# Slots taken behind the second sequence's last output product, constant rows made in the first stage, two expert loads inside the block stage

## The chip, the cores and the metric

The kernel runs on one core of one Trainium2 chip. The metric is device time in microseconds (us) of one execution. The kernel before has a median of 1152.28 us over three runs (1148.9, 1152.95, 1152.28). Engines are named as the profile names them: PE is TensorE (matrix products and transposes), PEld its weight loads, DVE is VectorE, ACT is ScalarE, POOL is GpSimd, SP is SyncE, which here only issues DMAs. A name such as "ACTq" is the same engine's queue of issued DMAs.

## The reference

The input x has shape (8, 512, 512): eight sequences of 512 tokens of width 512, all in float32. What is computed, cut to what matters:

```python
xn = layernorm(x)

# (a) lightning attention: 16 heads of 32, chunks of 128 tokens, a decay per head
q, k, v = rotary(silu(xn @ Wq)), rotary(silu(xn @ Wk)), xn @ Wv
per chunk:
    scores  = (q k^T) * D                      # D: decay inside the chunk, causal
    o       = scores v + (q * decay_q) S
    S       = lam_C * S + (k * decay_k)^T v    # state carried to the next chunk
gate = xn @ Wg1 @ Wg2
o    = o * sigmoid(gate)
o    = o * rsqrt(mean over each head of o^2 + eps) * norm_weight
s    = o @ Wo

# (b) mixture of experts over all 4096 tokens, 16 experts, top 4, hidden width 128
p     = softmax(xn @ gate_w.T);  keep the 4 largest, scaled to a sum of 1
mixed = sum over the 4 experts e of  p_e * (silu(xn Wg_e) * (xn Wu_e)) Wd_e
share = sigmoid(xn @ shared_gate_w) * swiglu(xn; sWg, sWu, sWd)
g     = silu(mixed + share)

out = x + s * g
```

## The kernel before

**Stages.** All of x is first normalised, and written to DRAM by token (`xn_d`) and transposed (`xT_d`). Every token is routed to four experts; an expert computes only its own tokens, in blocks of 128 that may hold tokens of any sequence. The stages in order of time are:

1. *First stage* (0 to about 226 us): `first()` (L999) runs the norm, the transposes, the router and the shared expert for all eight sequences, a piece at a time between the products of sequence 0 of the attention. `sort()` (L375) counts, and gives each of the 4 x 4096 choices its position in the lists of experts. It leaves `posi` (stored to `at_d`) and `sp` (the position's upper and lower part in float16).
2. *Table* (226 to about 302 us): beside sequence 1 of the attention, `table(room)` (L483) turns positions around: which token stands at each place of each of the 143 blocks. For each group of 16 choices DVE makes two one-hot tables, `place` and `block` (`make`, L529, L532, L535), by comparing a row of counting numbers `count` with `sp`; ACT scales half of the rows by the token's number (`number`, L543), DVE scales the other half by `half_token`. PE multiplies the two tables into `pn` (L566), and DVE adds the eight `pn` into `acc` (L575). At the end PE folds `acc` with the matrix `fold` into `pslot` (L582), and DVE makes the integer `slot` of it (L586). This is the list that the gathers read.
3. *Blocks* (about 321 to 710 us): 56 pairs of blocks and then 24 single blocks, always done (136 in all, `SURE`); up to 7 more stand in an If (L1280) behind them. For each block POOL gathers its 128 token rows by `slot` (L1112), SP transposes half of each row by DMA (`turn_rows`, L1119), PE the other half (`transpose_x`), ACT copies both into `xts` (`join`, L1138 and L1142; those of pair 0 by DVE), DVE copies the expert's weights to `wst` and the tokens' router weights to `w` (`prepare`, L1161, L1163), PE computes gate and up (`gate_up`, L1180, tile `pgu`), ACT the silu (L1192), DVE the product with up (L1193), PE the down product (`down`, L1211, tile `py`), DVE scales it (L1215) and SP stores it to `y_d` (L1216).
4. *Late stage* (about 710 to 1153 us): the attention of sequences 2 to 7. For each tile the four expert rows of a token are gathered from `y_d`, added up and multiplied in.

**Experts' weights.** `wexp` holds 16 experts of 768 KB each in SBUF. SP loads experts 0 to 10 at the start of the table stage (L1063). The room of the last five (`LATE`) is where the table works: one pair of `place` and `block` (`homes[0]`) in the room of experts 11 and 12, with `count` behind it, which reaches a little into expert 13's; the other pair in that of experts 14 and 15, with `half_token`, `fold` and `acc` behind it. So experts 11 to 13 are issued on SP when the table's last group is made (L556), each as the rows in its room are done with, and experts 14 and 15 on ACT's queue when the table is finished (L1077). Which expert a block reads is known only at run time, by a register (`of_block`, read from `eoff`), so an instruction that reads `wexp` counts as a reader of any expert.

**The turn from sequence 1 to the blocks.** `sequence(1, ...)` takes one step of the table at each `between[0]()`, called behind every product matmul of `value` (L618) and `product` (L662). With n == FIRST (2) its tail is: `gate_1(2)` (L629, PE, tile `pg`), `squares(1)` (L781 ACT squares, L784 PE sums, tile `pr`, L788 ACT square root), `inverse` (L792, DVE, `rs`), `value(2, 3)` (L615, tile `pv`) and `normed(1)` (PE spreads `rs` as `pb`, L801, and DVE scales the attention's output `on`, L806). What the table still has to do comes behind that. Then come the gathers of the first three pairs, `experts_of_blocks` (L1256 to L1263, six DVE operations that make `eoff`, in the room of `xts`), the four projections of sequence 1 (`project`, L813, tile `pw`, four tiles of four matmuls, 32 rows in the records), their copies (`spill`, L996 ACT, L997 store), and `begin(0, ...)` (L1218), which also issues `gate_2(2)` (L645) ahead of the first pair.

**Order.** The instructions of an engine are put in order by a scheduler, except where the code pins them: `on_pe()` (L208) places a matmul behind the one traced before it, and `behind(engine)` (L216) places an instruction behind the last one traced on that engine. `gone` is the list of DVE instructions that `prepare` is pinned to. SBUF comes from pools; a tile that takes the room of an older one waits for that one's readers. The pool `att` holds the tag `tmp` in `TMP` = 4 turns (`y`, `so`, `g1`, `rs` and the silu parts of q and k), and `v`, `kT`, `qT`, `xT`, whose room the blocks use again as `more`, `pls`, `wst` and `xts`. `p1` holds the first stage's tiles and is given up for `wexp`; `const` lives to the end. The gathered rows have six homes in turn, three `xg` of a pool of the blocks' own and three slices of `more`.

```python
    for t in range(NC):
        spill(FIRST - 1, t, project(FIRST - 1, t))
    on_of.pop(FIRST - 1)
    begin(0, lambda: gate_2(FIRST, banks="aakd"))
    by_dve.clear()
    blocks(range(len(items) + 2), aside)
```

## Time and profile before

| what | value |
|---|---|
| runs | 1148.9, 1152.95, 1152.28 us; median 1152.28 |
| profiled execution | 1155.04 us; its span, first to last instruction, 1153.2 us |
| mean granted TensorE clock | 0.99 of full |
| PE busy | 1117.9 us, 97% of the span, 7670 matmuls |
| DVE, ACT, POOL busy | 736.7, 429.3, 446.8 us (64, 37, 39%) |
| DMA | 218.49 MB, mean 189 GB/s |

By stage, from the table of busy time in stretches (us; the clock is the share of full speed that PE was granted):

| stretch | length | PE | DVE | ACT | POOL | clock | DMA engines' share |
|---|---|---|---|---|---|---|---|
| 0 to 226, first stage | 226 | 213.85 | 135.64 | 77.31 | 42.63 | 1.00 | 0.54 |
| 226 to 320, table | 94 | 82.50 | 66.76 | 36.69 | 12.39 | 0.93 | 0.62 |
| 320 to 710, blocks | 390 | 389.70 | 186.51 | 151.75 | 120.86 | 1.00 | 0.94 |
| 710 to 1153, late stage | 443 | 431.85 | 347.77 | 163.55 | 270.90 | 0.99 | 0.47 |

How to read it: the span is the profiled execution from its first to its last instruction; the execution itself was 1.84 us longer. A row of the trace in order of time begins with the start and the duration in us, then the engine, the line of the kernel, the operation, the tile written and the tiles read, the shapes and the number of instructions that the row joins; a bracket at its end is the engine's idle time just before it and what ended that. DMA rows under an engine's queue ("SPq", "ACTq", "POOLq") are the moments at which the engine issues them.

### The profile page before, as it was taken

Reading aid. Unit: us, or ns where it says so; the run is one execution under the profiler, and the core shown is the slowest. Engines: PE = TensorE matmul, PEld = TensorE weight load, DVE = VectorE, ACT = ScalarE, POOL = GpSimd, SP = SyncE. Lnnn points to the kernel's source line nnn. Section 1 sums busy time; section 2 is a strip of 40 time slices with the busy share of each in tenths; the row PEclk is TensorE's granted clock in tenths of the full one; section 3 lists DMA queues with packets and bytes.
Section 4 is the critical chain, followed back from the end, with each engine's and each line's share of the span. In section 5 each row is a group of like instructions: output and inputs, shape, how many; then the busy total and the mean of one; then the engine's idle time right before and its main releaser. Section 6 shows DMA issues by size and latency. Waiting matters only on the chain. (4 is left out here: it accounts for less than half of the span.)

```text
span 1153.2 us, 21330 instructions
## 1 busy us (share of the span) xinstructions
PE 1117.9 (97%) x7670; PEld 679.7 (59%) x7670; DVE 736.7 (64%) x1580; ACT 429.3 (37%) x927; POOL 446.8 (39%) x427
## 2 busy tenths in 40 slices
PE   7999999989899999999999999999999999999998
PEld 4445554445477777777777775555645545545554
DVE  6358734899334444555444445968879597697784
ACT  3223424154253333333333342353351522522541
POOL 3213100300233333333333322764877857958211
PEclk9999999989999999999999999999999999999999
DMA  9975431191799999999999994833737637434012
GB/s 338 319 276 194 156 127 47 51 352 40 217 200 236 220 244 238 238 241 237 253 233 234 272 215 178 323 101 108 254 116 230 183 108 244 150 122 145 29 36 75
DMA packets 163931, 218.49 MB, mean 189 GB/s; under 512 B 89840, under 2 KB 99184, under 8 KB 161776
## 3 DMA queue, kind: packets, MB, share of 16 engines
q1 hardware_dynamic: 142416, 145.18, 40.5%
q0 software_dynamic: 21120, 70.34, 23.9%
q10 hardware_dynamic: 288, 1.57, 0.4%
q8 instruction: 63, 1.03, 0.4%
q14 instruction: 44, 0.36, 0.1%
HBM read 126.78 MB, written 72.43 MB: 173 GB/s over the span
## 5 line engine op out<-in xcount | busy, mean ns | idle before, releaser
L1180 PE MATMUL pgu<-xts,wst 128*128 128x256 f32 x896 | 204.3, 381 | 0.0
L1180 PEld LDWEIGHTS pgu<-xts,wst 128*128 128x128 f32 x896 | 171.3, 191 | 46.7 <-issue 13.4
L1112 POOL DMA_INDIRECT xg<-xn_d,slot x69 | 65.7, 953 | 229.4 <-DVE w L1163 118.4
L1313 POOL DMA_INDIRECT yg<-y_d,place x128 | 142.5, 1113 | 31.1 <-issue 18.5
L1215 DVE TENSOR_SCALAR y<-py,w 128x512 f32<-128x512 f32 x136 | 101.6, 750 | 44.7 <-PE py L1211 31.0
L1211 PE MATMUL py<-wexp,slb 128*128 x272 | 129.9, 593 | 0.0
L615 PE MATMUL pv<-wv,xT 128*128 128x512 f32 x256 | 120.1, 610 | 3.1 <-DMA xT<-xT_d 2.0
L659 PE MATMUL pq<-xT,wq 128*128 128x512 f32 x256 | 118.2, 604 | 0.3 <-PEq L1278 0.3
L659 PE MATMUL pk<-xT,wk 128*128 128x512 f32 x256 | 118.2, 603 | 0.0
L1192 ACT ACTIVATE slb<-pgu 128x256 f32<-128x256 f32 (+1 forms) x80 | 28.1, 351 | 222.5 <-PE pgu L1180 184.1
L813 PE MATMUL pw<-wo,on 128*128 128x512 f32 x224 | 103.9, 612 | 5.8 <-DVE m L1351 5.8
L1193 DVE TENSOR_TENSOR slb<-slb,pgu 128x256 f32<-128x256 f32 (+1 forms) x80 | 30.5, 381 | 119.5 <-ACT slb L1192 118.1
L1112 POOL DMA_INDIRECT more<-xn_d,slot x67 | 63.5, 948 | 93.1 <-DVE w L1163 56.9
L1355 POOL TENSOR_TENSOR xo<-xo,m 128x512 f32<-128x512 f32 x31 | 45.3, 1460 | 131.2 <-DVE m L1351 123.3
L1142 ACT COPY xts<-pl 128x512 uint16<-128x512 uint16 x110 | 84.1, 767 | 9.0 <-DMA pl<-xg 9.0
L659 PEld LDWEIGHTS pq<-xT,wq 128*128 128x128 f32 x256 | 48.1, 193 | 55.3 <-issue 53.9
L748 DVE TENSOR_TENSOR sc<-ps,dmask 128x512 f32<-128x512 f32 x128 | 79.0, 676 | 0.9 <-PE ps L723 0.9
L615 PEld LDWEIGHTS pv<-wv,xT 128*128 128x128 f32 x256 | 46.3, 191 | 53.7 <-issue 47.1
L813 PEld LDWEIGHTS pw<-wo,on 128*128 128x128 f32 x224 | 42.5, 196 | 57.1 <-issue 47.7
L659 PEld LDWEIGHTS pk<-xT,wk 128*128 128x128 f32 x256 | 46.2, 189 | 50.7 <-issue 48.3
L1161 DVE COPY wst<-wexp 128x512 f32 x112 | 42.8, 424 | 39.8 <-DVE y L1215 18.7
L1211 PEld LDWEIGHTS py<-wexp,slb 128*128 128x128 f32 x272 | 45.5, 191 | 27.4 <-issue 26.8
(196 smaller groups left out, 1716.5 us busy)
## 6 DMA issues: line engine op xcount, KB each, us to landing
y_d<-y SPq DMA_DIRECT2D x136, 256.0 KB
wexp<-in_experts SPq DMA_DIRECT2D x14, 768.0 KB
sh_d<-sh SPq DMA_DIRECT2D x32, 256.0 KB
xT<-xT_d SPq DMA_DIRECT2D x8, 1024.0 KB
m<-sh_d SPq DMA_DIRECT2D x32, 256.0 KB
xo<-in_x SPq DMA_DIRECT2D x32, 256.0 KB
out<-xo SPq DMA_DIRECT2D x31, 256.0 KB
x<-in_x SPq DMA_DIRECT2D x7, 1024.0 KB
```

Of the source, the lines that this page charges most:

```text
L615: nc.tensor.matmul(pv, lhsT=xT_of[b][:, k, t * P : (t + 1) * P], rhs=wv[:, k, :], start=(k == 0), stop=(k == KC - 1))
L659: nc.tensor.matmul(ps, lhsT=w[:, k, g * P : (g + 1) * P], rhs=xT_of[b][:, k, :], start=(k == 0), stop=(k == KC - 1))
L748: nc.vector.tensor_tensor(s, pss[j].rearrange("p (c t) -> p c t", t=C), dmask[:, g * HG + j].unsqueeze(1).to_broadcast([P, NC, C]), ALU.mult)
L813: nc.tensor.matmul(pw, lhsT=on_of[b][:, g, t * P : (t + 1) * P], rhs=wo[:, g, :], start=(g == 0), stop=(g == G - 1))
L1112: nc.gpsimd.indirect_dma_start(out=row(i), out_offset=None, in_=xn_d, in_offset=bass.IndirectOffsetOnAxis(ap=slot[:, i : i + 1], axis=0))
L1142: (nc.vector.tensor_copy if j in by_dve else nc.scalar.copy)(xt[:, u, KP:, :].bitcast(U16).rearrange("p k (t h) -> p h k t", h=2), pls[j % ...
L1161: nc.vector.tensor_copy(to, wflat[:, bass.ds(off + u * KC * F, KC * F)])
L1180: nc.tensor.matmul(pg[:, o * 2 * P : (o + 1) * 2 * P], lhsT=wst[j % 2][k // KP][:, (k % KP * 2 + o) * F :][:, :F], rhs=xt[:, :, k, :], sta ...
L1211: nc.tensor.matmul(py, lhsT=hT[:, u * P : (u + 1) * P], rhs=wflat[:, bass.ds(off + KC * 2 * F, D)], start=True, stop=True)
L1215: gone.append(nc.vector.tensor_scalar(y, py, w[:, u : u + 1], None, ALU.mult).ins)
L1313: nc.gpsimd.indirect_dma_start(out=yg, out_offset=None, in_=y_d, in_offset=bass.IndirectOffsetOnAxis(ap=place[:, r, g : g + 1], axis=0))
L1355: nc.gpsimd.tensor_tensor(xo, xo, m, ALU.add)
```

## The change

- `TMP` goes from 4 to 5.
- `posi` moves from the first stage's pool to `const`. `count`, `half_token` and `fold` get tiles of their own in `const`, and are made on POOL in the first stage, behind `halves(0)`; the table no longer makes them (three ACT copies and the iota on POOL at its start) and no longer keeps them in `wexp`'s room.
- In the tail of sequence 1 four steps of the table are taken before `gate_1(2)`, and the next one behind it, so that the last `pn`, `pslot` and `slot` come behind the last output product; `slot` is pinned in DVE's order.
- `experts_of_blocks` moves ahead of `value(2, 3)` and `normed(1)`, works in the room of `wexp` from expert 14 on in place of `xts`, and is pinned in DVE's order. `prepare` is pinned behind the last scaling of `normed` (`scaled`).
- Experts 14 and 15 are no longer loaded on ACT's queue at the table's end; SP issues them inside the block stage, behind the gate and up of pairs 1 and 3 (`aside`).
- The homes of gathered rows swap halves, so that the first three are slices of `more`; the gathers are pinned on POOL, the DMA transposes chained in the order written, and the two copies of transposed halves in `join` pinned behind the copy before them.

```diff
--- before.py
+++ after.py
@@ -35,7 +35,7 @@
 
 NB = (B * N * TOPK + E * (P - 1)) // P
 WE = KC * 2 * F + D
-TMP = 4
+TMP = 5
 FIRST = 2
 NBQ = -(-NB // 4)
 
@@ -189,10 +189,13 @@
 
     wt = p1.tile([P, NT, E], F32, tag="wt", name="wt")
     sgs = p1.tile([P, NT], F32, tag="sgs", name="sgs")
-    posi = p1.tile([P, TOPK, NT], I32, tag="posi", name="posi")
+    posi = const.tile([P, TOPK, NT], I32, tag="posi", name="posi")
 
     sp = const.tile([P, 2, TOPK * NT], F16, tag="slot", name="sp")
 
+    count = const.tile([P, 2 * NB, QUAD], F16, tag="count", name="count")
+    half_token = const.tile([P, NT], F16, tag="half_token", name="half_token")
+    fold = const.tile([P, HALF], F16, tag="fold", name="fold")
     eoff = const.tile([P, 2, NBQ], I32, tag="eoff", name="eoff")
     end = const.tile([P, 2, E], F32, tag="end", name="end")
     filled = const.tile([P, 1], I32, tag="filled", name="filled")
@@ -497,7 +500,6 @@
                 flat.rearrange("p (u q j) -> p u q j", u=quads, j=QUAD))
 
         homes = [(part(quads, HALF, QUAD), part(quads, 2 * NB, QUAD))]
-        count = part(2 * NB, QUAD)
         free[0] = 2 * WE * (LATE - LATE // 2)
         homes.append((part(quads, HALF, QUAD), part(quads, 2 * NB, QUAD)))
 
@@ -505,13 +507,7 @@
             free[0] += n
             return half[:, free[0] - n : free[0]]
 
-        half_token, fold, acc = flat(NT), flat(HALF), flat(2 * NB)
-        nc.scalar.copy(half_token, token)
-        for h in range(0, P, HALF):
-            nc.scalar.copy(fold[h : h + HALF], ident[h : h + HALF, h : h + HALF])
-        nc.gpsimd.iota(
-            count, [[1, 2 * NB], [0, QUAD]], base=0, channel_multiplier=0,
-            allow_small_or_imprecise_dtypes=True)
+        acc = flat(2 * NB)
 
         def rows(of, n):
             return of.rearrange("p (u j) -> p u j", j=QUAD).unsqueeze(2).to_broadcast(
@@ -583,7 +579,8 @@
                     pt[h * HALF : (h + 1) * HALF, :NB], lhsT=fold,
                     rhs=acc.rearrange("p (b h) -> p b h", h=2)[:, :, h], start=True, stop=True)
         t = const.tile([P, NB], I32, tag="slot", name="slot")
-        nc.vector.tensor_scalar(t, pt[:, :NB], float(B * N // 2), None, ALU.add)
+        with behind(DVE):
+            nc.vector.tensor_scalar(t, pt[:, :NB], float(B * N // 2), None, ALU.add)
         slots.append(t)
 
 
@@ -791,6 +788,8 @@
     def inverse(b):
         nc.vector.reciprocal(rs_of[b], rs_of[b])
 
+    scaled = []
+
     def normed(b):
         pbs = [bank("a", f"pb_{b}_{c}") for c in range(NC)]
         rs = rs_of.pop(b)
@@ -803,8 +802,8 @@
                         rhs=rs[cq, :], start=True, stop=True)
         for c in range(NC):
             oc = on_of[b][:, :, c * C : (c + 1) * C]
-            nc.vector.tensor_tensor(
-                oc, oc, pbs[c].rearrange("p (g t) -> p g t", t=C), ALU.mult)
+            scaled[:] = [nc.vector.tensor_tensor(
+                oc, oc, pbs[c].rearrange("p (g t) -> p g t", t=C), ALU.mult).ins]
 
     def project(b, t):
         pw = bank("d", f"pw_{b}_{t}")
@@ -826,6 +825,27 @@
         by_token(b, 0)
         query(b, 1)
         step()
+
+    def experts_of_blocks():
+        half = NBQ * 2 * E
+        room = wflat[:, (E - LATE // 2) * WE :]
+        cm = room[:, :half].rearrange("p (b e) -> p b e", e=2 * E)
+        ef = room[:, half : half + NBQ]
+        ei = room[:, half + NBQ : half + 2 * NBQ].bitcast(I32)
+        with behind(DVE):
+            nc.vector.tensor_tensor(
+                cm, end.rearrange("p w e -> p (w e)").unsqueeze(1).to_broadcast([P, NBQ, 2 * E]),
+                iota_b.unsqueeze(2).to_broadcast([P, NBQ, 2 * E]), ALU.is_le)
+        with behind(DVE):
+            nc.vector.tensor_reduce(ef, cm, axis=AX.X, op=ALU.add)
+        with behind(DVE):
+            nc.vector.tensor_copy(ei, ef)
+        with behind(DVE):
+            nc.vector.tensor_scalar(ei, ei, E - 1, None, ALU.bitwise_and)
+        with behind(DVE):
+            nc.vector.tensor_scalar(eoff[:, 0], ei, float(WE), None, ALU.mult)
+        with behind(DVE):
+            nc.vector.tensor_scalar(eoff[:, 1], ei, float(D), None, ALU.add)
 
     def sequence(b, step, projected, before=None, defer=False, also=lambda: None):
 
@@ -867,9 +887,13 @@
             step()
         v_of.pop(b)
         if n == FIRST:
+            for _ in range(4):
+                next(filling)
             gate_1(n)
+            next(filling, None)
             squares(b)
             inverse(b)
+            experts_of_blocks()
             value(n, 3)
             normed(b)
             return
@@ -1026,6 +1050,15 @@
     turn(0)
     norm(1)
     halves(0)
+    with behind(POOL):
+        nc.gpsimd.tensor_copy(half_token, token)
+    for h in range(0, P, HALF):
+        with behind(POOL):
+            nc.gpsimd.tensor_copy(fold[h : h + HALF], ident[h : h + HALF, h : h + HALF])
+    with behind(POOL):
+        nc.gpsimd.iota(
+            count, [[1, 2 * NB], [0, QUAD]], base=0, channel_multiplier=0,
+            allow_small_or_imprecise_dtypes=True)
     xs_of.pop(0)
     load_x(3)
     pieces = first()
@@ -1069,12 +1102,8 @@
     next(filling)
     between[0] = lambda: next(filling, None)
     sequence(1, lambda: None, spill)
-    for _ in filling:
-        pass
     between[0] = lambda: None
     slot = slots[0]
-    for e in range(E - LATE // 2, E):
-        nc.scalar.dma_start(wexp[:, e, :], a["experts"][:, e, :])
     left.close()
 
 
@@ -1085,8 +1114,8 @@
     ROW = 2 * (D + E)
     HOMES = 6
     more = att.tile([P, 2 * NC * D], U16, tag="v", name="more", bufs=2)
-    homes = [blkp.tile([P, ROW], U16, tag=f"xg{j}", name=f"xg{j}") for j in range(HOMES // 2)]
-    homes += [more[:, j * ROW : (j + 1) * ROW] for j in range(HOMES // 2)]
+    homes = [more[:, j * ROW : (j + 1) * ROW] for j in range(HOMES // 2)]
+    homes += [blkp.tile([P, ROW], U16, tag=f"xg{j}", name=f"xg{j}") for j in range(HOMES // 2)]
     pls = [att.tile([P, 2, KC, P], U16, tag="kT", name=f"pl{j}", bufs=2) for j in range(2)]
     xts = att.tile([P, 2, 2, KC, P], F32, tag="xT", name="xts", bufs=1)
     wst = [
@@ -1099,6 +1128,7 @@
         {}, {}, {}, {}, {}, {}, [], [], [])
 
     by_dve = [0]
+    turned = []
 
     def inside(f):
         return lambda j: f(j, items[j]) if 0 <= j < len(items) else None
@@ -1109,14 +1139,17 @@
     @inside
     def gather(j, its):
         for i in its:
-            nc.gpsimd.indirect_dma_start(
-                out=row(i), out_offset=None, in_=xn_d,
-                in_offset=bass.IndirectOffsetOnAxis(ap=slot[:, i : i + 1], axis=0))
+            with behind(POOL):
+                nc.gpsimd.indirect_dma_start(
+                    out=row(i), out_offset=None, in_=xn_d,
+                    in_offset=bass.IndirectOffsetOnAxis(ap=slot[:, i : i + 1], axis=0))
 
     @inside
     def turn_rows(j, its):
         for u, i in enumerate(its):
-            nc.sync.dma_start_transpose(pls[j % 2][:, u], row(i)[:, D : 2 * D])
+            with tc.issue_after(turned[-1]) if turned else nullcontext():
+                turned.append(nc.sync.dma_start_transpose(
+                    pls[j % 2][:, u], row(i)[:, D : 2 * D]).ins)
 
     @inside
     def transpose_x(j, its):
@@ -1139,9 +1172,10 @@
             xt[:, :, :KP, :].rearrange("p u k t -> p u (k t)"),
             pt_of.pop(j)[:, : n * KP * P].rearrange("p (u kt) -> p u kt", u=n))
         for u in range(n):
-            (nc.vector.tensor_copy if j in by_dve else nc.scalar.copy)(
-                xt[:, u, KP:, :].bitcast(U16).rearrange("p k (t h) -> p h k t", h=2),
-                pls[j % 2][:, u].rearrange("p (h k) t -> p h k t", h=2))
+            with behind(DVE if j in by_dve else ACT):
+                (nc.vector.tensor_copy if j in by_dve else nc.scalar.copy)(
+                    xt[:, u, KP:, :].bitcast(U16).rearrange("p k (t h) -> p h k t", h=2),
+                    pls[j % 2][:, u].rearrange("p (h k) t -> p h k t", h=2))
         xt_of[j] = xt
 
     def on_dve(what, i, low, high):
@@ -1242,32 +1276,20 @@
                 down(j - 1)
 
     def aside(j):
+        if j in (1, 3):
+            e = E - LATE // 2 + j // 2
+            nc.sync.dma_start(wexp[:, e, :], a["experts"][:, e, :])
         if j == PAIRS:
             load_xT(FIRST)
 
     kept.clear()
 
-    def experts_of_blocks():
-        half = NBQ * 2 * E
-        room = xts.rearrange("p j u k t -> p (j u k t)")
-        cm = room[:, :half].rearrange("p (b e) -> p b e", e=2 * E)
-        ef = room[:, half : half + NBQ]
-        ei = room[:, half + NBQ : half + 2 * NBQ].bitcast(I32)
-        nc.vector.tensor_tensor(
-            cm, end.rearrange("p w e -> p (w e)").unsqueeze(1).to_broadcast([P, NBQ, 2 * E]),
-            iota_b.unsqueeze(2).to_broadcast([P, NBQ, 2 * E]), ALU.is_le)
-        nc.vector.tensor_reduce(ef, cm, axis=AX.X, op=ALU.add)
-        nc.vector.tensor_copy(ei, ef)
-        nc.vector.tensor_scalar(ei, ei, E - 1, None, ALU.bitwise_and)
-        nc.vector.tensor_scalar(eoff[:, 0], ei, float(WE), None, ALU.mult)
-        nc.vector.tensor_scalar(eoff[:, 1], ei, float(D), None, ALU.add)
-
     for j in range(3):
         gather(j)
-    experts_of_blocks()
     for t in range(NC):
         spill(FIRST - 1, t, project(FIRST - 1, t))
     on_of.pop(FIRST - 1)
+    gone += scaled
     begin(0, lambda: gate_2(FIRST, banks="aakd"))
     by_dve.clear()
     blocks(range(len(items) + 2), aside)
@@ -1279,6 +1301,7 @@
         items[:] = [(i,) for i in range(SURE, NB)]
         done.clear()
         gone.clear()
+        turned.clear()
         for j in range(3):
             gather(j)
         begin(0)
```

## The prediction on record

> **What bounds the kernel now.** The first part of the page has PE busy for 1117.9 of 1153.2 us (97%), and the chain that ended last runs mostly through PE. So I ask of each edit only where it moves a hole in PE's row, and what a hole costs behind it. I listed PE in order of time and looked for bracketed idle time, then read the engine named there, then the granted clock. These are PE's holes near the change (start, us, engine, line, tiles; the bracket is the idle time before and its releaser), with undisturbed rows of the same work for comparison:
>
> ```profile
> 237.35 0.90 PE L691 MATMUL pk<-ident,kT 128*128 128x128 f32 x3 [4.16 <-DVE state L738]
> 238.04 5.19 PE L659 MATMUL pq<-xT,wq 128*128 128x512 f32 x6
> ...
> 255.54 0.49 PE L691 MATMUL pk<-ident,kT 128*128 128x128 f32 x3
> 255.87 2.74 PE L659 MATMUL pq<-xT,wq 128*128 128x512 f32 x6
> ...
> 265.92 4.54 PE L615 MATMUL pv<-wv,xT 128*128 128x512 f32 x6 [2.02 <-DMA xT<-xT_d]
> ...
> 283.33 2.84 PE L615 MATMUL pv<-wv,xT 128*128 128x512 f32 x6
> ...
> 300.83 0.26 PE L582 MATMUL pslot<-wexp 128*64 128x143 f16 x2 [2.76 <-DVE on L806]
> 301.01 15.67 PE L813 MATMUL pw<-wo,on 128*128 128x512 f32 x32
> ...
> 319.88 1.15 PE L645 MATMUL p<-g,wg 32*128 32x128 f32 x26 [1.90 <-ACT so L996]
> 320.97 5.41 PE L1180 MATMUL pgu<-xts,wst 128*128 128x256 f32 x16
> ...
> 326.65 3.62 PE L1180 MATMUL pgu<-xts,wst 128*128 128x256 f32 x16
> ```
>
> Each of these four holes is paid twice: the same matmuls behind it take longer. In the table by stretches the granted clock reads 0.50 from 237 to 243 and from 267 to 270. Holes of 1.90 to 4.16 us cost 1.7 to 2.9 us behind them; one of 1.16 us at 868.87 cost nothing (its eight pw took the usual 3.70).
>
> The causes, on the other engines and queues:
>
> ```profile
> 226.21 3.24 POOL L512 IOTA wexp<- 128x572 f16 x1 [9.01 <-DMA at_d<-posi]
> ...
> 229.48 0.43 DVE L529 TENSOR_TENSOR wexp<-wexp,sp 128x512 f16<-128x512 f16 x1 [4.42 <-POOL wexp L512]
> ...
> 301.12 0.33 ACTq L1077 DMA_DIRECT2D wexp<-in_experts  x1
> 305.13 0.76 DVE L1161 COPY wst<-wexp 128x512 f32 x2 [2.17 <-DMA wexp<-in_experts]
> 318.01 1.38 ACT L1142 COPY xts<-pl 128x512 uint16<-128x512 uint16 x2 [7.53 <-DMA pl<-xg]
> ```
>
> The reader sees that the table's first DVE row waits for the iota, the iota for a store; and that the hole at 319 comes from ACT standing in a wait for a transpose with two evictions queued behind it. From 321 us on PE has no hole for 56 pairs of 5.61 us, with the DMA engines 0.93 busy (500 to 700 us): what the start of that stage gains or loses goes straight to the end.
>
> **1. Rows made early (gain 6.1).** DVE's last list cast ends at 225.06. The table then started at 229.48; without the iota, the three ACT casts and the store's release (posi now has a home of its own) it can start at 225.1, 4.4 earlier. Its ten operations take 7.1 us, so the state copies come at 232.2 instead of 236.5, ahead of PE, whose keys end at 233.18. The idle 4.16 goes, and with it 0.90-0.49 and 5.19-2.74, together 2.86 of slow clock: 7.0. What is late next: bank a for gate_2, freed by the eviction of the first pn, which on DVE stands behind kT and half of the next table rows. I get PE waiting until 240.2 for it, about 1.4 where it lost 0.6 before, so 0.9 back: 6.1 (bounds 5.0 and 7.0). The moved copies and the iota stand on POOL behind halves(0), some 4 to 5 us (3.24 for the iota); POOL is idle there for 5.83 us before 25.03, so they cost nothing; without that cover, at most the time by which the next rstd would be late, some 1 us.
>
> **2. A third expert ahead of xT (loss 2.8).** With count gone from the shared room, expert 13's load depends on no table row, and in the built program SP issues it ahead of sequence 2's xT. xT is wanted sooner too: PE's scores end at 257.8 (263.9 less 6.1). Expert 13 waits for expert 10's landing, which I put at 254.6 (257.2 less the 2.6 by which SP's fourth load comes forward). Both transfers, 1.84 MB, then go together: the three loads at 287.41 moved 2.36 MB in 7.1 us, which gives 5.8 for these, and about 1 us of older stores is in front, so xT lands near 262.1. The hole grows from 2.0 to 4.3; the slow clock behind it by 0.5, between the rows' 1.7 and 2.9. Bounds: 0 (xT lands 5.1 after its issue, as now) and 4.
>
> **3. Slots and norm behind the last po (gain 2.6).** Now, last po (289.13) to first pw (301.01) is 11.9 us. After: pn 1.15, pg 1.0, pslot 0.3, pr 1.0 on PE (3.4); ACT's table load and root end at 4.2; reciprocal 0.95; experts_of_blocks, now ordered ahead of the scaling, 1.36+1.35+4x0.18 = 3.4 (8.6); first scaled tile 0.6: pw starts at 9.3. PE's own work, pv 3.6 and pb 1.17, ends at 8.1, so a hole of 1.2 remains where 2.76 was. Expert 11 and 12's loads at table end come with the same shift.
>
> **4. The projections' clock (gain 1.9).** 15.67 for 32 pw against 32x0.43 = 13.74. The remaining hole of 1.2 is nearest to the row of 1.16, which kept its clock. Bounds 0 and 1.9.
>
> **5. No wait at gate_2 (gain 3.7).** slot is now ready about 2.8 us behind the last po instead of 13.6, so gathers and transposes have landed some 10 us before the projections end; ACT runs the four evictions first and DVE copies pair 0's transposes. The 1.90 goes and 5.41-3.62 = 1.8. If a transpose still were late here, the 3.7 would stay as it is.
>
> **6. Experts 14 and 15 inside the pairs (loss 7.2).** This is the new wait. The loads leave ACT's queue, where only DVE's 2.17 waited for them, and go to SP at blocks 1 and 3. The expert is chosen by register, so a reader of wexp behind such a load waits for it whole: in the built program the first py waits for 14's semaphore, and the third py, put in the middle of the fifth pair's pgu, for 15's. PE is in order, so all pgu behind wait too. From the first pgu: load 14 waits for pair 2's weight copies (3.45 for pgu 0, 0.6 for the copy) and is issued at 4.2. By the row at 301.12 such a load lands 3.6 us after its issue, at 7.9; py is due at 7.8. In front of it in SP's order are two transposes, beside it two pairs of gathers, so I add 1.7: a stall of 1.8, and 1.8 for the clock, as behind 1.90: 3.6. Bounds: 0.1, and 7.2 (landing 7.9 after the issue, as pair 0's transposes from 307.45 to 315.3, and 2.9 of clock). Load 15 waits for py of pair 1, then for y and pair 4's weight copies; two transposes and two stores of y precede it. It is issued about 10 us behind py 0, due 13 behind it: again 3.6, bounds 0.4 and 7.2. Behind SP's waiting load stand the transposes of pairs 4 and 7, due 10 us or more later. The rest (TMP of 5, order of the homes, transposes chained, ACT's copy order) lies beside PE: ACT waits 183.6 us for pgu in this stage, and PE's order is unchanged from pair 5 on. Bounds -2 and 1, at nothing: no PE row there names a tmp buffer.
>
> On the clock, the Trainium skill, "TensorE: Matmul & The Clock Gate", section "HAM oscillation — how this bites in real kernels", says that holes are dangerous above about 3.4 us. By that the stalls of 1.8 would keep their clock, but the slow rows behind 1.90 and 2.76 would not exist either; the trace shows them, and decides. By the page item 6 would be 3.6 and items 4 and 5 together 1.9, a sum of 4.2.
>
> **Sum.** 6.1-2.8+2.6+1.9+3.7-7.2 = 4.3 us earlier. The profiled execution took 1155.04 (span 1153.2 and 1.84 around it), so 1150.7 for it; the median shown is 2.76 lower, and I take the same off: 1152.28-4.3 = **1148.0**.
>
> **Rivals.** A, the loads land in time: item 6 is 0.5 instead of 7.2, gain 11.0, 1141.3. For it: 3.6 us at 301.12; against it: the DMA engines were free then and are 0.93 busy here. B, the gains are eaten: xT 4 late and both stalls near 3.2 with 2.4 of clock, gain 6.1-4+2.6+1.9+3.7-11.2 = -0.9, 1153. Also here: the table is DVE-bound (it has almost no idle time from 229 to 262), so item 1 comes out smaller. C, slower: the 1.57 MB, some 4 us of all DMA engines, don't fit into a stage with 0.4 us free per pair. Then transposes land late for six pairs or so, each a hole of 1.2 with up to 1.8 behind it: 4.3-18 = 13.7 later, 1166, down to 1158 if the clock holds. It decides once a transpose lands over 8 us after its issue (507.71, read from 515.7); now no pair waits for one.
>
> **Chances.** Forecast (1145 to 1150.5) 0.46, A (below 1145) 0.24, B 0.18, C 0.12. A change of 0.5%, 5.8 us, is about what a measurement of this kernel can tell from none: below 1146.5 lie A and 0.17 of the forecast: faster 0.41; slower, above 1158, C: 0.12; within 0.47. The ends: all best, 14.7 gained; items at their worst, 6 lost. The range 1140 to 1156 leaves out C and a third of A.
>
> **What would show it.** Item 1: no hole before L691 near 233, the iota before 25 us. 2: a hole of 4 us before pv near 262. 3: pslot about 2 us behind the last po, pw 9.3 behind. 4: 32 pw in 13.9. 5: the first pgu 2.6 behind the last pw and 3.6 long. 6: holes before the first and third py, released by wexp's loads, with slow rows behind. I am wrong if py waits for neither load, if xT lands by 260, or if holes come up in the steady pairs.

## The result, and the profile after

The changed kernel takes 1164.33 us (median of four runs, 1163.86 to 1168.53) against 1152.47 for the kernel before: ratio 1.0115, 95% interval 1.0088 to 1.0142. It is **slower by 12 us**, where 4.3 us less were forecast. Its profiled execution took 1164.48, with a span of 1162.7, so the two profiles to compare differ by 9.5 us.

PE's rows of the kernel after in order of time, those that answer to the ones shown of before (start, us, engine, line, tiles; in brackets the idle time before and its releaser; L812 is the L813 of before, L1214 the L1180, L1245 the L1211):

```profile
233.25 0.55 PE L688 MATMUL pk<-ident,kT 128*128 128x128 f32 x3 [0.24 <-DVE state L735]
...
264.86 5.49 PE L612 MATMUL pv<-wv,xT 128*128 128x512 f32 x6 [7.25 <-DMA xT<-xT_d]
...
288.08 1.08 PE L767 MATMUL po<-sc,v 128*32 128x128 f32 x32
...
291.26 0.26 PE L578 MATMUL pslot<-wexp,fold 128*64 128x143 f16 x2
...
298.61 14.00 PE L812 MATMUL pw<-wo,on 128*128 128x512 f32 x32 [1.34 <-DVE on L805]
...
314.72 3.69 PE L1214 MATMUL pgu<-xts,wst 128*128 128x256 f32 x16
...
327.48 3.75 PE L1245 MATMUL py<-wexp,slb 128*128 x4 [4.73 <-DMA wexp<-in_experts]
331.02 4.16 PE L1214 MATMUL pgu<-xts,wst 128*128 128x256 f32 x16
...
335.46 1.88 PE L1245 MATMUL py<-wexp,slb 128*128 x4
...
347.31 3.78 PE L1245 MATMUL py<-wexp,slb 128*128 x4 [4.35 <-DMA wexp<-in_experts]
...
654.37 2.07 PE L1220 MATMUL pgu<-wexp,xt 128*128 x4 [3.46 <-ACT xt L1176]
```

The reader sees: the hole ahead of the keys is gone; the one ahead of `pv` has grown from 2.02 to 7.25; `pslot` comes 2.1 us behind the last `po`, and the projections run at full clock; the pairs begin 6.25 us earlier than before (314.72 against 320.97). Then two `py` wait for `wexp`, and the matmuls behind them take twice their 1.88. A hole among the single blocks, at 654, is one nobody had reckoned with.

SP's queue tells when the loads were issued:

```profile
255.71 0.33 SPq L552 DMA_DIRECT2D wexp<-in_experts  x1
256.44 0.32 SPq L594 DMA_DIRECT2D xT<-xT_d  x1
...
316.75 3.49 SPq L1151 DMA_TRANSPOSE pl<-more  x2
320.34 0.53 SPq L1281 DMA_DIRECT2D wexp<-in_experts  x1
...
341.23 0.38 SPq L1281 DMA_DIRECT2D wexp<-in_experts  x1
```

Laid against each other, the two profiles give this account. "Pairs" runs from the first `pgu` to the first `pgu` of a single block, "singles" from there to the first `pq` of the late stage.

| step of the prediction | forecast | measured | from |
|---|---|---|---|
| 1, rows early | +6.1 | +6.3 | sequence 1's last scores end 257.61, before 263.90 |
| 2, expert 13 ahead of xT | -2.8 | -6.3 | the last `po` ends at 289.1 in both |
| 3, tail | +2.6 | +2.4 | first `pw` 298.61, before 301.01 |
| 4, clock of `pw` | +1.9 | +1.7 | 14.00, before 15.67 |
| 5, gate_2 | +3.7 | +3.9 | rest of the 6.25, and 3.69 for 5.41 |
| 6, two loads in the pairs | -7.2 | -14.5 | pairs 326.53, before 313.75 less that 1.72 |
| "the rest", at nothing | 0 | -6.5 | singles 81.61, before 75.14 |
| late stage, not in the sum | 0 | +3.5 | 439.84, before 443.34 |
| sum | +4.3 | -9.5 | |

The last row but one is no gain of the change: before's profiled execution had a hole of 2.61 us in the late stage with 5.34 for eight `pw` behind it, which is 1.15 and 3.70 after, and that execution was 2.8 us above its kernel's median. The fifth `tmp` buffer alone changes nothing (e10 below).

### The profile page after: what moved, and what is told of

Read it like the earlier page. It is cut to its first block, busy times and chain, and to the rows that moved or that the text cites. A ratio compares the mean times of both kernels' runs of the same rounds, so it can differ in the third digit from the quotient of the medians.

```text
span 1162.7 us, 21323 instructions
## 1 busy us (share of the span) xinstructions
PE 1117.9 (96%) x7670; PEld 679.6 (58%) x7670; DVE 738.6 (64%) x1580; ACT 437.0 (38%) x924; POOL 447.5 (38%) x430
## 5 line engine op out<-in xcount | busy, mean ns | idle before, releaser
L1214 PE MATMUL pgu<-xts,wst 128*128 128x256 f32 x896 | 204.2, 381 | 0.1
L1214 PEld LDWEIGHTS pgu<-xts,wst 128*128 128x128 f32 x896 | 171.3, 191 | 47.8 <-issue 27.0
L1143 POOL DMA_INDIRECT more<-xn_d,slot x69 | 66.0, 956 | 246.1 <-DVE w L1197 113.5
L1245 PE MATMUL py<-wexp,slb 128*128 x272 | 134.7, 611 | 9.1 <-DMA wexp<-in_experts 9.1
L656 PE MATMUL pq<-xT,wq 128*128 128x512 f32 x256 | 115.7, 593 | 0.3 <-PEq L1300 0.3
L812 PE MATMUL pw<-wo,on 128*128 128x512 f32 x224 | 100.6, 596 | 5.9 <-DVE m L1374 4.5
L1143 POOL DMA_INDIRECT xg<-xn_d,slot x67 | 63.3, 945 | 100.4 <-DVE w L1197 61.3
L1176 ACT COPY xts<-pl 128x512 uint16<-128x512 uint16 x110 | 76.7, 767 | 0.7 <-DMA pl<-more 0.7
L812 PEld LDWEIGHTS pw<-wo,on 128*128 128x128 f32 x224 | 41.2, 190 | 55.3 <-issue 45.2
L1245 PEld LDWEIGHTS py<-wexp,slb 128*128 128x128 f32 x272 | 46.7, 196 | 38.2 <-issue 33.3
```

Source lines behind the costliest of these rows:

```text
L656: nc.tensor.matmul(ps, lhsT=w[:, k, g * P : (g + 1) * P], rhs=xT_of[b][:, k, :], start=(k == 0), stop=(k == KC - 1))
L812: nc.tensor.matmul(pw, lhsT=on_of[b][:, g, t * P : (t + 1) * P], rhs=wo[:, g, :], start=(g == 0), stop=(g == G - 1))
L1143: nc.gpsimd.indirect_dma_start(out=row(i), out_offset=None, in_=xn_d, in_offset=bass.IndirectOffsetOnAxis(ap=slot[:, i : i + 1], axis=0))
L1176: (nc.vector.tensor_copy if j in by_dve else nc.scalar.copy)(xt[:, u, KP:, :].bitcast(U16).rearrange("p k (t h) -> p h k t", h=2), pls[j % ...
L1214: nc.tensor.matmul(pg[:, o * 2 * P : (o + 1) * 2 * P], lhsT=wst[j % 2][k // KP][:, (k % KP * 2 + o) * F :][:, :F], rhs=xt[:, :, k, :], sta ...
L1245: nc.tensor.matmul(py, lhsT=hT[:, u * P : (u + 1) * P], rhs=wflat[:, bass.ds(off + KC * 2 * F, D)], start=True, stop=True)
```

## The experiments

Theory S: the loss is made of waits, py's for the loads inside the pairs and pv's for xT. Rival T: the traffic of the loads costs, wherever it is put. Each group ran on one chip. On that of the first group the kernel before took 1152.5 us; on the four chips of the others 1163.4 to 1164.1, so there only ratios count. Most of that difference lies in the late stage, behind nearly all that is edited here: 439 to 444 us in the first group's profiles and in the two above, 451 to 458 in all others. A ratio is to the kernel before of the same group, with its 95% interval. From each profile, in us:

| kernel | ratio | first pgu at | pairs | singles |
|---|---|---|---|---|
| before | 1 | 320.97 | 313.75 | 75.14 |
| after | 1.0115 (1.0088 to 1.0142) | 314.72 | 326.53 | 81.61 |
| e1 loads on ACT | 0.9996 (0.9967 to 1.0025) | 318.95 | 312.03 | 75.22 |
| e2 xT first | 1.0091 (1.0065 to 1.0116) | 311.39 | 323.24 | 81.27 |
| e3 both | 0.9989 (0.9972 to 1.0006) | 317.90 | 312.03 | 76.08 |
| e4 traffic only | 1.0009 (0.9993 to 1.0024) | 319.21 | 312.03 | 77.11 |
| e5 xT first, loads on SP | 1.0004 (0.9985 to 1.0023) | 310.58 | 316.88 | 78.11 |
| e6 zeros behind xT | 0.9968 (0.9943 to 0.9994) | 310.63 | 318.19 | 79.92 |
| e7 tail alone | 0.9995 (0.9965 to 1.0025) | 317.73 | 313.69 | 75.28 |
| e8 loads at pair 20 | 1.0110 (1.0085 to 1.0135) | 315.28 | 327.65 | 77.92 |
| e9 loads on ACT, late | 1.0001 (0.9978 to 1.0025) | 312.63 | 315.43 | 79.70 |
| e10 before, TMP 5 | 0.9995 (0.9977 to 1.0012) | 319.33 | 314.40 | 75.14 |
| e11 orders undone | 1.0134 (1.0109 to 1.0158) | 325.18 | 323.72 | 75.14 |
| e12 after again | one run, 1183.77 us | 314.70 | 328.73 | 80.87 |
| e13 after, pin out | 1.0030 (1.0002 to 1.0057) | 312.84 | 326.27 | 76.29 |
| e14 before, pin in | 1.0038 (1.0004 to 1.0071) | 319.51 | 316.14 | 80.02 |
| e15 e9, pin out | 0.9897 (0.9842 to 0.9953) | 312.95 | 313.69 | 75.62 |
| e16 after, third profile | 1.0089 (1.0066 to 1.0112) | 313.85 | 323.16 | 82.28 |
| e17 before, other pin | 1.0043 (1.0013 to 1.0073) | 318.32 | 318.17 | 77.32 |
| e18 e15 again | 0.9929 (0.9905 to 0.9953) | 311.29 | 313.77 | 75.79 |

### Group 1: the stalls, xT and the traffic

e1: the two loads leave the pairs.

```diff
 def aside(j):
-    if j in (1, 3):
-        e = E - LATE // 2 + j // 2
-        nc.sync.dma_start(wexp[:, e, :], a["experts"][:, e, :])
...
 slot = slots[0]
+for e in range(E - LATE // 2, E):
+    nc.scalar.dma_start(wexp[:, e, :], a["experts"][:, e, :])
```

> Experts 14 and 15 go back to ACT's queue at the table's end; all else is the changed kernel. Theory S (stalls): the two waits of py for wexp (4.73 and 4.35 us) and the slow clock behind each are what the block stage lost; they go, 14.5 us less than the changed kernel's 1164.3, so 1150 (1147 to 1153). Theory T (traffic): the 1.57 MB cost their time wherever they are moved, by lateness of the transposes that follow; then holes appear at the first pairs instead and the time stays above 1157. The hole of 3.46 us among the single blocks: if it belongs to the change it is seen here too.

e2: expert 13 behind xT.

```diff
+with tc.issue_after(xT_load[FIRST]):
     nc.sync.dma_start(wexp[:, e, :], a["experts"][:, e, :])
```

> Expert 13's load is held behind the load of sequence 2's xT on SP; all else is the changed kernel. Theory S: xT lands some 5.1 us behind its issue as in the kernel before, the hole ahead of pv is near 4.4 instead of 7.25, and the slow clock behind it is shorter: 3 to 4.5 us less than the changed kernel, 1160.5. Rival: xT waits for the stores of zeros issued ahead of it, not for expert 13; then the hole stays above 6.5 and the time at 1164.

e3 is e1 and e2 together.

> Both edits together. Theory S: the gains add, 18 to 19 us below the changed kernel: 1146 (1143 to 1149), 6 us below the kernel before. Theory T: above 1155.

e4 is e1, and in `aside` at pairs 1 and 3 a load of the same bytes into DRAM, `nc.sync.dma_start(spare[j // 2], ...)`, pinned behind the last transpose.

> As the first of these, experts 14 and 15 on ACT's queue at the table's end, but two loads of the same size are issued by SP at the places where the changed kernel issues those of experts 14 and 15; they copy the same bytes to a room in DRAM that nobody reads, so no instruction waits for them (their result is not used). Theory S: no py hole; within 2 us of the first kernel, 1150 to 1152. Theory T: the traffic alone makes transposes late, 1157 or more.

Measured: e1 took 1151.53 (12.8 less than the changed kernel), e2 1161.16, e3 1149.91, e4 1153.98. In e1, e3 and e4 no py waits, and the pairs take 312.03 in all three, with the traffic and without: 326.53 - 312.03 = 14.5 is what the two waits cost. T falls: e4 is 0.0013 above e1, inside the intervals; its 1153.98 is 2 us over what S gave, and in its profile 1.9 of them stand among the single blocks, none in the pairs. e2 is 3.2 us under the changed kernel, as S gave; one of its py waits 3.69 for the load, at the other PE stands 3.89 where the profile names nothing that it waited for. e3 is above the 1143 to 1149 that S gave, since ACT's queue has a price of its own; ACT's rows of e1:

```profile
290.14 2.79 ACTq L1108 DMA_DIRECT2D wexp<-in_experts  x1
292.97 1.28 ACT L785 ACT_TABLE_LOAD   x1 [2.92 <-issue]
```

and PE's of the same:

```profile
263.73 5.12 PE L612 MATMUL pv<-wv,xT 128*128 128x512 f32 x6 [5.92 <-DMA xT<-xT_d]
...
295.76 1.17 PE L800 MATMUL pb<-rs,wge 16*128 16x128 f32 x32 [1.26 <-DVE rs L789]
299.85 16.98 PE L812 MATMUL pw<-wo,on 128*128 128x512 f32 x32 [2.92 <-DVE on L805]
```

The load's issue stood 2.8 us in front of the square root; the norm came late, and `pw` took 16.98 for 14.00. The hole ahead of pv is 4.88 in e2 and 5.50 in e3, 5.92 and 5.80 in e1 and e4: expert 13 explains only a part of the 7.25, 2.4 between the changed kernel and e2, 0.4 between e1 and e3.

### Group 2: where the rest of xT's wait comes from, and where a load may stand

e5 is e3 with `nc.sync` for `nc.scalar`. e6 is e5 with the stores of zeros behind xT:

```diff
-for i in range(SURE, NB):
-    nc.sync.dma_start(y_d[i * P : (i + 1) * P, :], none)
...
+for b in range(SURE, NB):
+    with tc.issue_after(xT_load[FIRST]):
+        nc.sync.dma_start(y_d[b * P : (b + 1) * P, :], zeros[0])
```

e7 is the kernel before with the tail's order and the two loads on SP at the table's end. e8 is the changed kernel with both loads in `aside` at `j == 20`.

> The changed kernel with expert 13 behind xT, and experts 14 and 15 issued by SP at the table's end instead of inside the pairs (before, with ACT's queue, the load stood ahead of ACT's square root and cost a hole of 1.3 ahead of pb, 1.6 more ahead of pw and 3.0 of slow clock). Theory: no hole ahead of pb, pw 14.0, no py hole; 5.9 us less than the same with ACT's queue (1149.9): 1144 (1141.5 to 1146.5). Rival: the two loads stand ahead of pair 0's transposes on SP and make pgu 0 late by some 4 us: 1148 or more.

> As e5, and the seven stores of zeros (1.84 MB) are issued behind xT too, from a tile of their own. Theory D: the DMA engines are full from 228 to 260 us, so xT can't land before what stands ahead of it has; without these stores it lands at 258 to 259.5 instead of 262.5, the hole ahead of pv is 1 to 2 us instead of 5, and the clock behind it is shorter: 4 us less than e5, 1140 (1137.5 to 1142). Rival: xT's landing is set by its own issue (it waits for PE's last reads of sequence 1's xT) and takes 5 us or more whatever is ahead: the hole stays above 4, the time within 1.5 us of e5.

> The kernel before with one part of the change alone: the order of the tail (last pn, pslot, slot directly behind the last output product, experts of blocks ahead of the norm), and experts 14 and 15 issued by SP at the table's end. The rows stay in the table. Theory: the tail's three terms, 2.4 + 1.7 + 3.9 = 8.0 measured between the two profiles, come without the early rows: 1152.5 - 8 = 1144.5 (1142 to 1147), and e5 is within 2 us of it, since the early rows alone only make PE wait longer for xT. Rival: the early rows are worth their 6 us, then this is 6 us above e5.

> The changed kernel with both loads issued one behind the other at pair 20 instead of pairs 1 and 3. Theory S: a py waits wherever the load is put; one hole near pair 21, as long as two loads take to land (8 to 10 us) less the some 3 us by which py is due later, so 5 to 7 and 2.5 of slow clock, and no py hole at the first pairs: 14.5 - 9 = 5.5 us less than the changed kernel, 1159 (1156 to 1161). Rival: the stalls belong to the crowded start of the stage; in its middle the loads land in time, no py hole, 1150.

PE and SP of e6, and then of e8 (two views each; the first row of each fence is PE's):

```profile
260.25 2.84 PE L617 MATMUL pv<-wv,xT 128*128 128x512 f32 x6 [2.88 <-DMA xT<-xT_d]
```

```profile
254.31 0.33 SPq L598 DMA_DIRECT2D xT<-xT_d  x1
254.69 4.72 SPq L553 DMA_DIRECT2D y_d<-none  x7
```

```profile
446.26 3.75 PE L1245 MATMUL py<-wexp,slb 128*128 x4 [7.52 <-DMA wexp<-in_experts]
```

```profile
436.38 1.16 SPq L1281 DMA_DIRECT2D wexp<-in_experts  x2
```

e6 has the hole at 2.88 without slow clock, where theory D gave 1 to 2 and its rival more than 4. Its ratio is 0.0036 under e5's (3.7 us by the medians), with intervals that overlap, and in the two profiles the first pgu comes at the same time, since PE stands 2.92 ahead of `pw` in e6 where the profile names nothing. So D has the direction, not the size: from issue to landing xT takes 5.94 us in e6 and 6.95 in e5. The stores ahead of xT were a part of its wait.

e8 shows py waiting 7.52 in the middle of the stage, so the wait is not one of a crowded start. Its pairs are 15.6 us longer than e1's. By PE's rows 10.5 of them are that wait and the slow clock behind it, and 4.8 a wait of the second pgu for ACT (3.11) with its clock, which the first chip's profiles don't have. So both loads at once cost 4 us less than apart, where S gave 5.5; the ratio, with the other wait in it, doesn't show it.

e5 and e7 missed: neither is 8 us under the kernel before, though they are within 1 us of each other, as e7's theory had it. In e7 the hole ahead of `pw` is 2.94 and `pw` takes 15.70, so its first pgu comes only 1.6 us earlier than e10's. Part of the loss is the second pgu's wait, of these later chips: 3.09 for ACT in e5, 2.08 in e10 (an unchanged kernel but for one buffer), 1.39 in e7 with nothing named. e5's pairs begin 8.75 us before e10's; it gives back 2.5 in the pairs and 3.0 in the singles (78.11). Its profiled execution, 1158.78, was the fastest of its ten; what the median of 1164.43 lost beyond that isn't shown.

### Group 3: the parts inside the block stage

e9 is e6 with the two loads on ACT's queue, each under `with behind(ACT):`, behind the copy of v. e10 is `TMP = 5` in the kernel before. e11 is the changed kernel with old homes, gathers, transposes and copies (`behind` and `turned` taken out of `gather`, `turn_rows` and `join`). e12 is the changed kernel.

> The changed kernel with xT ahead of expert 13 and of the stores of zeros (as e6), and experts 14 and 15 on ACT's queue again, but behind ACT's square root and the copy of v, so that nothing that PE needs stands behind them. Theory: hole ahead of pv under 3 us, pw with a hole near 1.3 and 14.0 to 15.7 us, no hole ahead of the second pgu (3 us and 1.6 of clock in e5 and e6, where SP's loads stood between the transposes): 4 us under e6, whose ratio to the kernel before was 0.9968, so 0.993 (0.990 to 0.996). Rival: the loads take the DMA engines from pair 0's and pair 1's transposes wherever they are issued from; 0.997 or more.

> The kernel before with five turns of the buffer tmp instead of four, nothing else. The late stage took 431.7 us in the profile before and 428.1 in the one after, from the same instruction on. Theory L: the fifth turn does that, ratio 0.997 (0.996 to 0.998), the late stage near 428 on a chip like the first. Rival: it was one hole of 2.6 us in the profiled execution, by chance; ratio 1.000 within its interval.

> The changed kernel with the orders inside the block stage as before (homes of gathered rows, gathers and transposes not chained, copies of transposed halves not pinned); the loads of experts 14 and 15 stay inside the pairs. The stage of single blocks took 75.1 us before and 81.6 after, 6.5 of it a hole of 3.46 and its slow clock. Theory O: the pinned orders make transposes late there; this is 5 to 6 us below the changed kernel, ratio 1.006. Rival: late transposes there are chance or follow the loads inside the pairs; ratio within 0.002 of the changed kernel's 1.0115.

> The changed kernel once more, for a second profile. The two py holes (4.73 and 4.35) and the hole ahead of pv (7.25) belong to the change and come again within 1 us; the hole among the single blocks, if it is chance, is missing or elsewhere, and then the span is some 6 us less against the kernel before.

e10 is no different from before. e9 missed its 0.993 widely: 79.70 for the singles, 3.18 ahead of `pw` with nothing named, and again 3.13 of ACT ahead of the second pgu, which its theory had put down to SP's loads. e11 missed in its ratio (1.0134, within its rival's bounds) and hit in its stage: the singles take 75.14 again, although the loads are inside the pairs; its loss lies in the tail, where DVE now stood for pair 0's transposes ahead of the norm. DVE's and PE's rows of e11:

```profile
302.14 0.46 DVE L1175 COPY xts<-pl 128x512 uint16<-128x512 uint16 x1 [4.55 <-DMA pl<-xg]
...
305.16 0.45 DVE L1175 COPY xts<-pl 128x512 uint16<-128x512 uint16 x1 [2.29 <-DMA pl<-xg]
```

```profile
306.42 16.65 PE L812 MATMUL pw<-wo,on 128*128 128x512 f32 x32 [9.03 <-DVE on L805]
```

So DVE's pin in `join` earns its place. e12, a single execution of 1183.77, has the hole of pv (6.58), one of py (7.05; at the first load a wait of 3.12 for ACT had already held PE) and four small ones among the singles. So the waits are not an accident of one execution; that both py holes come again within 1 us was wrong.

### Groups 4 and 5: one pin

In the built programs the pins on gathers and transposes move nothing: without these alone all five engines keep the changed kernel's order. What is left is the pin on ACT's copies. e13 takes it out of the changed kernel from pair 2 on, e14 puts it alone into the kernel before, e15 is e9 without it from pair 2 on (the pins on gathers and transposes go there too, from pair 3 on), e16 the changed kernel beside them:

```diff
-            with behind(DVE if j in by_dve else ACT):
+            with behind(DVE if j in by_dve else ACT) if j < 2 else nullcontext():
```

> The changed kernel without one pin: from pair 2 on, ACT's copies of transposed halves are not pinned behind the copy of pt, and ACT's order there is that of the kernel before (one pl, pt, the other pl); SP differs in the place of a single transpose, no other engine differs. In the profiles so far the stage of single blocks took 75.1 to 75.3 us in all four kernels with the old order and 75.2 to 81.6 in all ten with the pinned one (mean 78.7). Theory A: the pinned order does it; the stage takes 75.1 to 75.5 here, and the time is 3 to 6 us below the changed kernel in this call. Rival: what makes transposes late there are the loads inside the pairs or chance; 77 to 82 again, time within 2 us.

> The kernel before with that pin added, nothing else (ACT's order from pair 0 on: pt, pl, pl; SP one transpose elsewhere, no other engine differs). Theory A: the stage of single blocks takes 76.5 to 81 us instead of 75.1, ratio to the kernel before 1.001 to 1.005. Rival: 75.1 again, ratio 1.000 within 0.0015.

> The ninth kernel (xT ahead of expert 13 and of the stores of zeros, experts 14 and 15 on ACT's queue behind the copy of v) without the pin from pair 2 on. Theory A: its stage of single blocks took 79.7 and takes 75.1 to 75.5 here, so 3 to 5 us below the ninth's 1.0001: ratio 0.9955 to 0.998. Rival: 0.9990 or more.

> The changed kernel in the same call, so that the others are compared with it on the same chip, and for one more profile. The theory of the stalls gives again one or two py holes of 4 to 7.5 us and 1.010 to 1.017.

ACT's waits in the stage of single blocks (engine, line, what for: us in total, times, longest), first of before, then of e14:

```profile
ACT slb L1192 <- PE pgu L1186: 38.4, 23, 3.0
ACT xt L1142 <- DMA pl<-more: 3.3, 3, 2.1
ACT xt L1142 <- DMA pl<-xg: 1.4, 4, 0.5
```

```profile
ACT xt L1143 <- DMA pl<-xg: 17.0, 7, 5.3
ACT xt L1143 <- DMA pl<-more: 14.6, 7, 4.0
ACT slb L1193 <- PE pgu L1187: 12.3, 7, 2.4
```

Before, ACT waits for PE; with the pin it waits for transposes, 31.6 us in place of 4.7, and PE waits for ACT. e14 is 1.0038 with nothing but that, e13 is 0.0059 under e16 (which, at 1.0089 and with py holes of 1.49 and 5.51, is a little better than expected). Counted over all profiles: in seven profiles with the old order the singles took 75.14 to 76.29, in twelve with the pin 75.22 to 82.28, in the mean 79.2. Theory A holds, with two limits: e13's 76.29 is above its 75.1 to 75.5, and in e1 the singles took 75.22 with the pin, so it doesn't cost in every execution. e15 came out better than forecast, so it was run again (e18), and e17 asked whether the pin hurts by putting the copy of `pl` behind that of `pt`: in the kernel before, pinned as pl, pl, pt.

> The kernel before with ACT's copies pinned in the order pl, pl, pt instead of pt, pl, pl (the fourteenth kernel, which took 80.02 us for the single blocks and 1.0038 in all). Theory A': what costs is that the copy of pl stands behind that of pt, since SP issues the next transpose into the same room only when the copy of pl is done; the stage takes 75.1 to 76.3 and the ratio is 1.000 within 0.002. Rival: any pin does it; 77 to 82 again.

> The fifteenth kernel once more, with more rounds: it had 0.9897 (0.9842 to 0.9953) with few runs, more than its parts (4 to 5 us of the stage of single blocks) explain. If the gain belongs to the kernel, the ratio is 0.989 to 0.995 again and the stage 75.1 to 76.3; if it was the scatter of runs, 0.996 to 0.999.

e17's singles take 77.32, between the two; its ratio of 1.0043 has a hole of 4.15 in it, at the second pgu, behind an ACT that stood 3.94 ahead of gate_2's sigmoids; whether the pin made that one isn't shown, for e10 has 2.08 at this place without it. Neither answer fits, so **how** the pin delays the transposes stays open. What the rows show is that SP issues a transpose right behind ACT's copy out of the same room (before: copy 660.35 to 661.11, next transpose 661.14), of which there are two.

e18, the same kernel as e15, is at 0.9929 (0.9905 to 0.9953), 1155.9 against 1163.37: **0.7% faster than the kernel before**, where the changed kernel was 0.9% (e16) and 1.15% slower. PE's largest waits between the first stage and the late one, in e18:

```profile
PE pv L617 <- DMA xT<-xT_d: 3.3, 1, 3.3
PE pw L817 <- DVE on L810: 3.1, 1, 3.1
PE pgu L1221 <- ACT on L651: 1.5, 1, 1.5
```

No py and no single block waits any more; what remains of the change is its early rows, its tail and the orders of the first pairs.

## Why the prediction was wrong

Right, to within 0.3 us each: step 1 up to the scores, 3, 4 and 5. Step 4 had some luck: its clock held behind a hole of 1.34 here, and behind 1.84 in e8, at the same place, it did not. Three terms failed, and they made a gain of 4.3 into a loss.

**Step 6 was mis-sized by a factor of two.** The mechanism was as written: the first and the third py wait, whichever expert their pairs read (the loads stand behind pairs 1 and 3, not "blocks"). But load 14 stood behind two transposes until 320.34, 5.6 us behind the first pgu where I had 4.2, and landed 7.1 us after its issue where I had 3.6 and 1.7; py was due at 322.75. Load 15 was issued only 1.7 us ahead of its py, not 3. Each stall was 4.73 and 4.35 for 1.8, and the clock behind it cost 2.4 and 2.8 for 1.8. The row of 3.6 at 301.12 came from a time when the DMA engines did little else; I named the busy ones as what spoke against rival A and still took 5.3. The upper bound of 7.2 each came out, but by another sum: it had 7.9 from issue to landing, and the loads took 7.1 and 6.1 and were issued later.

**Step 2 had the wrong thing in front of xT.** I put "about 1 us of older stores" there and charged expert 13. Over all profiles the hole is 6.2 in the mean with expert 13 and the zeros ahead (eight profiles), 4.8 with expert 13 behind (e2, e3, e5), and 3.2 with both behind (e6, e9, e15, e18): each is worth some 1.5 us and its share of the clock. Expert 13 costs less by its traffic, which I charged, than by holding up SP: with it ahead xT is issued 1.1 us behind PE's last read of the old one, else 0.2, while from issue to landing it takes 8.3 in the mean and still 7.9 and 8.3 in e2 and e3 (6.95 in e5). Even with both behind, xT, which can be issued only when PE has read the last of sequence 1's, takes 5.9 us to land (e6). The rows by stretches of the kernel after (start and end; length; busy time of PE, PEld, DVE, ACT and POOL; clock, DMA engines' share, GB/s) show why:

```profile
235.00:245.00 10.00, 9.08 (x168) 6.07 (x167) 9.96 (x19) 5.94 (x15) 0.00 (x0) 1.00 1.00 403
245.00:255.00 10.00, 10.00 (x71) 4.84 (x73) 9.96 (x20) 5.39 (x16) 0.00 (x0) 1.00 1.01 370
```

The engines were full from 235 to beyond 255 with the eleven experts and the zeros. PE came 6.3 us earlier, xT only 1.06 (264.86 against 265.92), and the six pv behind the longer hole took 0.95 more: step 1's 6.3 us were given back to the last tenth. The Trainium skill has the rule that I missed, "DMA: Bandwidth & Descriptors", section "Queues, rings and completion order": on each DMA engine a queue's descriptors are taken in ring order; e6 agrees, xT landing 5.94 us after its issue with the stores issued behind it, 6.95 with them ahead (e5).

**"The rest ... at nothing" was wrong for one part.** I counted ACT's order of copies there because ACT waited 183.6 us for pgu. Those are the waits of the pairs alone; among the singles ACT waited 38.4 us for pgu, and although it had this slack, the order alone costs 4.9 (e14 against before) to 6.0 us (e16 against e13), since the transposes there are just in time and come later with it. The tmp buffer was rightly at nothing (e10).

Of the rivals, C gave the size (1158 to 1166) but not the cause: e4 has its traffic without its loss. With the clock held its six holes of 1.2 would by the way have come to 1155, not 1158, and the items at their worst to 7.1 lost, not 6. B had the cause of the first two terms, a later xT and longer stalls, but 4 and 11.2 us for the 6.3 and 14.5 measured, and so 1153. A fell at the first py.

## What to carry to other kernels

When an edit makes an engine ready earlier, ask for each transfer that it then meets what is queued ahead of it, in bytes over the measured rate, and move those bytes before counting the gain. A load into a tensor that is read by a register's index is a wait for every reader, wherever in a full loop it is put: it belongs in front of the loop, and in an engine's queue behind the steps that a norm waits for, not ahead of them. A pin that fixes an order needed at one place should not reach into a steady loop; put in alone, it shows its price.

## What the runs showed of the hardware

A hole's length alone does not decide the clock. Ahead of `pw`, 1.83 (e5) and 2.33 (e15) left 14.00 us, 1.84 (e8) made it 15.70; ahead of pv, 2.88 (e6) left six matmuls at 2.84, 2.02 (before) made them 4.54; ahead of the second pgu, 3.13 (e9) left it at 3.72, 3.11 (e8) made it 5.32. PE's rows of e5, then of e8:

```profile
294.68 14.00 PE L814 MATMUL pw<-wo,on 128*128 128x512 f32 x32 [1.83 <-DVE eoff L850]
```

```profile
297.47 15.70 PE L812 MATMUL pw<-wo,on 128*128 128x512 f32 x32 [1.84 <-DVE on L805]
```

The profile before has one of each kind in its late stage, and the prediction, by which holes from 1.90 on cost clock, left out the second:

```profile
946.20 5.34 PE L813 MATMUL pw<-wo,on 128*128 128x512 f32 x8 [2.61 <-DVE m L1351]
...
1025.87 3.70 PE L813 MATMUL pw<-wo,on 128*128 128x512 f32 x8 [1.91 <-DVE m L1351]
```

What decides besides the length, no run here shows.

On the chips of the later groups the kernel before took 1% more, and engines stood where the profile shows nothing to wait for ("issue"). ACT's row of e12, ahead of gate_2's sigmoids, where the first profile of the same kernel has no gap; in e5, e6 and e9 the gap is 3.35 to 3.60, in e16 and e18 1.9, and the second pgu waits behind it:

```profile
319.03 1.28 ACT L646 ACT_TABLE_LOAD   x1 [3.57 <-issue]
```

The Trainium skill, "Runtime: NRT & Kernel Launch", section "Instruction fetch mechanics", says that engines fetch their instructions by DMA in blocks, mostly hidden; no run here shows whether such a fetch was what ACT waited for.
